# A graph network on one core: ten open building steps with idle products, a later first one-hot, and other PSUM banks for the last matrices

## The chip, the cores and the metric

The kernel runs on one core of a Trainium2 chip. The metric is the device time of one launch in microseconds, given as the median of several runs.

## The reference, cut to what matters

```python
# N=6250 nodes, E=100000 edges sorted by dst, C=256, NOUT=64, 4 layers, all float32
def agg(h):
    return jax.ops.segment_sum(h[src], dst, num_segments=N)

x0 = x
x = jnp.maximum(_layernorm(x), 0.0)
for l in range(3):
    h = x + agg(x)
    h = relu(h @ W1s[l] + b1s[l])
    h = relu(h @ W2s[l] + b2s[l])
    x = h @ W3s[l] + b3s[l]
h = x + agg(x)
h = relu(h @ cW1 + cb1)
h = relu(h @ cW2 + cb2)          # 256 -> 64
return x0 + (h @ cW3 + cb3)      # 64 -> 256
```

## The kernel before

Nodes are handled in 49 blocks of 128 (`NT`). The first matrix of a layer is applied before the sum over edges, so each layer starts from a table `z = x @ W1` that lies in DRAM and, as a high and a low part side by side, in SBUF (`XY`, 128 x 49 x 512). The sum over edges is done in two ways. For one part of the blocks, rows are gathered by an indirect DMA (`rows`, line 1427) and summed by one-hot matrices `hot` (line 1450, built by VectorE) in short TensorE products; one such block is a *visit* (class `Gathered`; `add` does the visit, `one_hots` makes its `hot`). For the other 31 blocks (the list `made`) the kernel builds a dense matrix of edge counts, block by block, and multiplies it with `XY`. The last product of a layer for such a block is preceded by a cast of the counts from bytes to numbers that TensorE reads (`a`, line 1602 in layer 0, line 1618 later).

**Building.** `build` is a generator. One of its `yield`s is one *build*: two small TensorE products (line 1114) of a low one-hot `lo` and a high one-hot `hi` into a PSUM tile `bp` (three buffers), and one cast of `bp` into the byte matrix `at`, by ScalarE (line 1122) or VectorE (line 1124). `lo` and `hi` are made by VectorE for a batch of two builds, a batch ahead, two buffers each (line 1073), from `pairs`, which ScalarE copies. A block takes 16 builds; then VectorE adds the identity to its diagonal (line 1128) and the matrix is stored to DRAM for the later layers, which read it back. There are 496 builds in all.

**The order.** Everything is issued under a schedule written out by the program: `tick` advances a step counter `now`; `later(n, fn)` runs `fn` n steps on; `job` runs between two steps, and `queue` holds the second and third matrices of each team (`mlp`). Each engine runs its instructions in the order issued. Layer 0 starts with `PRE` *open steps*, which hold two builds each and no product; `PRE` follows from `EARLY`. After them each step of layer 0 multiplies four 128-column pieces (`product_by_node`, line 1642) and holds two builds or none: the list `goals` spreads what is left of the 496 builds evenly over the steps, from `GSUB + EARLY` on. Casts `a` are made `AHEAD` = 3 steps before their product. In the open steps ScalarE makes all casts of `bp`; after `2 * PRE` builds every second one is VectorE's. A model clock (`clock`, `passed`) paces the gathers and the visits.

Right before the open steps, `looked` ends with 16 products of 128 x 512 whose result is not read (line 862). Then `layers[0].begin()` makes the first visit's `hot`, eight gathers are sent, and the open steps run. The first product of the open steps needs `pairs`, `lo` and `hi`.

**The end.** In layer 3 (`l == NLAYER`) the matrices of a team are short: 256 to 64 (`second`) and 64 to 256 (`third`, or `halves` for a team of four, two PSUM tiles). `given_out` then adds the bias and the input `x`, which it loads for the last gathered block (a team of one, block 48) in place, on VectorE: first `xt` (lines 1304, 1307, or 1300 for the last panel), then, a step later, `zz` from PSUM (line 1317), and the store. PSUM tiles `ps` come from the pool `ps_m` with two buffers. The products over panels of four blocks take `agg` tiles from another pool, `ps_a`, which has four buffers in layers 1 to 3; a panel takes two, which line 1733 (ScalarE) and, for the last panel, line 1730 (VectorE) read. `hurry` is set for the last panel of a layer and for the last gathered block.

Of the kernel before, what the change touches and what calls it, by code (L numbers as in the profile page):

```python
# [17 lines left out]
P = 128  # L18
# [378 lines left out]
def sorted_edges(  # L397
# [603 lines left out]
    with tc.manual_schedule():  # L1001
# [179 lines left out]
        def tick(layer):  # L1181

            now[0] += 1
            run = [f for t, f in due if t <= now[0]]
            due[:] = [(t, f) for t, f in due if t > now[0]]
            for f in run:
                f()
            visit = layer.meets()
            for task in list(jobs):
                first, last, fn = task  # L1190
                if max(first, lock[0]) <= now[0] and (visit or last <= now[0]):
                    jobs.remove(task)
                    fn()
            if queue:
                step(visit)
# [54 lines left out]
        def mlp(l, b0, n, h1, hurry, far):  # L1250

            w = n * P
            end = l == NLAYER
            mid = NOUT if end else C
            mp = min(mid, P)
            soon = 1 if hurry else 2
            twin = end and n % 2 == 0
            h2 = []

            def second(i):  # L1260
                if i == 0:
                    h2.append(work.tile([P, KC, W], F32, name="h2"))
                ps = ps_m.tile([P, W], F32, name="ps")
                if twin:
                    v = w // 2
                    for c in range(KC):
                        for h in range(2):
                            mm = nc.tensor.matmul(ps[h * mp:(h + 1) * mp, :v], weights[l][0][:, c, :],
                                                  h1[:, c, h * v:(h + 1) * v], start=(c == 0),
                                                  stop=(c == KC - 1))  # L1270
                        passed(v * FULL32, mm)
                    later(soon, lambda: nc.scalar.activation(
                        h2[0][:, 0, :v], ps[:, :v], AF.Relu, bias=b2[l][:2 * mp, i:i + 1]))
                    return
                for c in range(KC):
                    mm = nc.tensor.matmul(ps[:mp, :w], weights[l][0][:, c, i * P:i * P + mp],  # L1276
                                          h1[:, c, :w], start=(c == 0), stop=(c == KC - 1))
                    passed(w * FULL32, mm)
                later(soon, lambda: nc.scalar.activation(h2[0][:mp, i, :w], ps[:mp, :w], AF.Relu,  # L1279
                                                         bias=b2[l][:mp, i:i + 1]))  # L1280

            def halves():
                m, w3 = n // 2, weights[l][1]
                pss = [ps_m.tile([P, W], F32, name="ps") for _ in range(2)]
                for q in range(m):
                    for h, ps in enumerate(pss):
                        k = slice(h * mp, (h + 1) * mp)
                        mm = nc.tensor.matmul(ps[:, q * C:(q + 1) * C],
                                              h2[0][k, 0, q * P:(q + 1) * P], w3[0][k, :],
                                              start=True, stop=True)  # L1290
                    passed(C * FULL32, mm)
                for h, ps in enumerate(pss):
                    given_out(h * m, m, ps)

            def given_out(i, m, ps):
                w3 = weights[l][1]
                if b0 in inputs:
                    xs = inputs[b0][i:i + m]
                    for t in xs:
                        nc.vector.tensor_tensor(t, t, w3[1], OP.add)  # L1300
                else:
                    xt = late.tile([P, 2, C], F32, name="xt", bufs=3)
                    if b0 + i + m == NT and LAST < P:
                        nc.vector.memset(xt[:, m - 1, :], 0.0)  # L1304
                    rows_io(x, b0 + i, m, xt, True)
                    xs = [xt[:, :m, :]]
                    nc.vector.tensor_tensor(xt[:, :m, :], xt[:, :m, :],  # L1307
                                            w3[1][:, None, :].to_broadcast([P, m, C]), OP.add)
                v = ps[:, :m * C].rearrange("p (q c) -> p q c", c=C)
                z = work.tile([P, 2, C], F32, name="zz", bufs=3)  # L1310

                def add():
                    each = m // len(xs)
                    for q, t in enumerate(xs):
                        o = slice(q * each, (q + 1) * each)
                        t = t if each == m else t[:, None, :]
                        nc.vector.tensor_tensor(z[:, o, :], v[:, o, :], t, OP.add)  # L1317

                later(soon, add)
                later(soon + 1, lambda: rows_io(out, b0 + i, m, z, False))  # L1320

            def third(i):
                m = min(2, n - i)
                w3 = weights[l][1]
                ps = ps_m.tile([P, W], F32, name="ps")
                for q in range(m):
                    nodes = slice((i + q) * P, (i + q + 1) * P)
                    o = ps[:, q * C:(q + 1) * C]
                    if end:
                        mm = nc.tensor.matmul(o, h2[0][:mp, 0, nodes], w3[0][:mp, :], start=True, stop=True)  # L1330
                    else:
                        for c in range(KC):
                            mm = nc.tensor.matmul(o, h2[0][:, c, nodes], w3[:, c, :],  # L1333
                                                  start=(c == 0), stop=(c == KC - 1))
                    passed((1 if end else KC) * C * FULL32, mm)
                if end:
                    given_out(i, m, ps)
                    return
                v = ps[:, :m * C].rearrange("p (q c) -> p q c", c=C)
                z = work.tile([P, 2, C], F32, name="zz", bufs=3)  # L1340
                later(soon, lambda: nc.vector.tensor_tensor(  # L1341
                    z[:, :m, :], v, w3[:, KC:, :].to_broadcast([P, m, C]), OP.add))

                def store():
                    rows_io(tables[l + 1], b0 + i, m, z, False)
                    blocks = range(b0 + i, b0 + i + m)
                    kept.update((l, j) for j in blocks)
                    if all((l, j) in used for j in blocks):
                        split(l, b0 + i, m, z)
                    else:  # L1350
                        for j in blocks:
                            reload(l, j)
                    if sum(1 for k, _ in kept if k == l) == NT:
                        layers[l + 1].begin()
                        later(1, lambda: load_weights(l + 1))

                later(2 * soon - 1, store)

            def seconds():
                passed(BURST)  # L1360
                for i in range(-(-mid // P)):
                    second(i)

            def thirds():
                passed(BURST)
                if twin:
                    halves()
                    return
                for i in range(0, n, 2):
                    third(i)  # L1370

            wait = 1 if hurry else far - 2
            queue.append(dict(steps=[seconds, thirds], since=now[0], first=now[0] + wait,
                              last=now[0] + wait + (0 if hurry else SPAN),
                              far=2 if hurry else far, hurry=hurry))


        class Gathered:
# [28 lines left out]
                    self.upto[self.done + 1] - self.upto[1]) * self.pace  # L1407

            def begin(self):
                self.one_hots(0)  # L1410
                self.end = begun[self.l] + work_of(self.l) - TAIL[self.l]
                self.pace = (self.end - clock[0] - MARGIN) / self.upto[-1]
                self.lead = MARGIN + self.upto[1] * self.pace
                self.first = clock[0] + self.lead
# [116 lines left out]
                                     pt[:, c, :len(us) * P], AF.Relu, bias=b1[l][:, c:c + 1])  # L1531


        EARLY = 8
        PRE = (GSUB + EARLY) // 2
        tails = [7] + [panels[-1][1] + gone[-1][1]] * (NLAYER - 1) + [panels[-1][1]]
        order = [[]] + [[0, 1, 2, 19, 3, 4, 5, 6]] * 2 + [[0, 17, 1, 18, 2, 3, 19, 4, 5, 6]]
# [210 lines left out]
        with tc.tile_pool(name="hots", bufs=1) as hots, tc.tile_pool(  # L1748
# [8 lines left out]
            layers[0].begin()  # L1757
            layers[0].send(8)
            beside = build(hots, ats, ps_b)
            while now[0] < PRE:  # L1760
                for _ in range(2):
                    next(beside)
                    built[0] += 1
                tick(layers[0])
                layers[0].advance()
            later(1, lambda: later(2, lambda bad=verdict(): judge(bad)))
# [76 lines left out]
```

## Time and profile before

| what | value |
|---|---|
| median of 3 runs | 2105.08 us (2103.89 to 2105.66) |
| profiled execution: time | 2104.15 us |
| profiled execution: span | 2102.4 us |
| mean granted clock | 0.996 |
| TensorE busy | 2031.7 us, 97% |
| VectorE, ScalarE, GpSimd busy | 933.8, 879.7, 1441.1 us |

Times are in microseconds from the start of the span. PE is TensorE, PEld its weight loads, DVE VectorE, ACT ScalarE, POOL GpSimd, SP SyncE, which issues most of the DMAs. A row `out<-in` names the tiles written and read, then shapes and count. The setup takes the first 115 us, layer 0 with the building lasts until about 640 us, and layers 1 to 3 take the rest.

### The profile page before, as it was taken

Reading aid. Unit: us, or ns where it says so; the run is one execution under the profiler, and the core shown is the slowest. Engines: PE = TensorE matmul, PEld = TensorE weight load, DVE = VectorE, ACT = ScalarE, POOL = GpSimd, SP = SyncE. Lnnn points to the kernel's source line nnn. Section 1 sums busy time; section 2 is a strip of 40 time slices with the busy share of each in tenths; the row PEclk is TensorE's granted clock in tenths of the full one; section 3 lists DMA queues with packets and bytes.
Section 4 is the critical chain, followed back from the end, with each engine's and each line's share of the span. In section 5 each row is a group of like instructions: output and inputs, shape, how many; then the busy total and the mean of one; then the engine's idle time right before and its main releaser. Section 6 shows DMA issues by size and latency. Waiting matters only on the chain. (4 is left out here: it accounts for less than half of the span.)

```text
span 2102.4 us, 33308 instructions
## 1 busy us (share of the span) xinstructions
PE 2031.7 (97%) x12117; PEld 1501.4 (71%) x12117; DVE 933.8 (44%) x2108; ACT 879.7 (42%) x1799; POOL 1441.1 (69%) x1450
## 2 busy tenths in 40 slices
PE   6889999999999999999999999999999999999997
PEld 4667666666667777777777777777777777777775
DVE  5987767767673422222233322222224333333333
ACT  5866656556555523322333432323333433323331
POOL 3747777777774377777777377777777377777773
PEclk9999999999999999999999999999999999999999
DMA  5544545545554654545556555555456455656554
GB/s 166 171 136 137 158 150 154 157 150 153 155 153 145 212 163 146 169 152 179 155 174 196 186 165 149 172 159 179 147 171 202 161 179 156 196 174 206 169 171 129
DMA packets 184324, 346.92 MB, mean 165 GB/s; under 512 B 32030, under 2 KB 118080, under 8 KB 184150
## 3 DMA queue, kind: packets, MB, share of 16 engines
q0 software_dynamic: 68144, 183.13, 29.9%
q1 hardware_dynamic: 114078, 159.72, 23.1%
q8 instruction: 97, 1.59, 0.3%
q10 hardware_dynamic: 1928, 1.85, 0.3%
q14 instruction: 77, 0.63, 0.1%
HBM read 286.50 MB, written 58.07 MB: 164 GB/s over the span
## 5 line engine op out<-in xcount | busy, mean ns | idle before, releaser
L1427 POOL DMA_INDIRECT rows<-table,idx x1377 | 1381.2, 1003 | 587.5 <-issue 225.4
L1720 PE MATMUL agg<-a,XY 128*128 128x512 f32 x4116 | 976.6, 394 | 1.9 <-DVE clT L1654 1.9
L1720 PEld LDWEIGHTS agg<-a,XY 128*128 128x128 f32 x4116 | 765.2, 188 | 190.1 <-issue 32.4
L1618 ACT CAST a<-at 128x512 fp32r<-128x512 uint8 (+1 forms) x549 | 332.7, 616 | 633.2 <-PE agg L1720 591.3
L1618 DVE CAST a<-at 128x512 fp32r<-128x512 uint8 (+1 forms) x550 | 251.0, 458 | 522.4 <-PE agg L1720 476.0
L1642 PE MATMUL agg<-XY,a 128*128 128x512 f32 x1519 | 420.9, 410 | 1.7 <-ACT a L1602 1.0
L1642 PEld LDWEIGHTS agg<-XY,a 128*128 128x128 f32 x1519 | 268.3, 189 | 54.2 <-issue 9.2
L1466 PE MATMUL sums<-rows,hot 128*32 128x256 f32 x3726 | 233.4, 381 | 8.7 <-DMA rows<-table,idx 8.5
L1122 ACT CAST at<-bp 128x392 uint8<-128x392 f32 x260 | 125.0, 489 | 188.8 <-PE bp L1114 182.6
L1466 PEld LDWEIGHTS sums<-rows,hot 128*32 128x32 f32 x3726 | 118.5, 109 | 117.1 <-issue 27.6
L1602 ACT CAST a<-at 128x512 fp32r<-128x512 uint8 (+2 forms) x362 | 197.5, 575 | 4.7 <-PE agg L1642 4.7
L1124 DVE CAST at<-bp 128x392 uint8<-128x392 f32 x236 | 132.8, 563 | 133.5 <-PE bp L1114 132.7
L1495 DVE TENSOR_TENSOR u<-u,sums 128x256 f32<-128x256 f32 x81 | 33.9, 419 | 265.3 <-PE agg L1720 241.9
L1114 PE MATMUL bp<-hi,lo 128*128 128x196 bf16 x992 | 129.5, 251 | 16.9 <-DVE hi L1073 16.1
L1073 DVE TENSOR_TENSOR hi<-cols,pairs 128x784 bf16<-128x784 bf16 x248 | 139.1, 561 | 0.0
L1333 PE MATMUL ps<-w,h 128*128 128x256 f32 x588 | 135.1, 382 | 1.4 <-ACT h L1279 0.9
L1276 PE MATMUL ps<-h,w 128*128 128x512 f32 (+3 forms) x332 | 133.7, 545 | 2.0 <-DVE zz L1317 1.7
L1114 PEld LDWEIGHTS <-lo 128*128 128x128 bf16 x992 | 72.8, 98 | 87.7 <-DVE hi L1073 37.3
L1333 PEld LDWEIGHTS ps<-w,h 128*128 128x128 f32 x588 | 112.4, 192 | 18.7 <-ACT h L1279 1.3
L1073 DVE TENSOR_TENSOR lo<-lanes,pairs 128x512 bf16<-128x512 bf16 x248 | 103.6, 418 | 0.2 <-issue 0.2
L1530 ACT ACTIVATE h<-ps,bias 128x256 f32<-128x256 f32 (+1 forms) x116 | 47.5, 464 | 134.1 <-PE ps L1526 134.1
L1341 DVE TENSOR_TENSOR zz<-ps,w 128x512 f32<-128x512 f32 (+1 forms) x75 | 50.2, 678 | 117.1 <-PE ps L1333 117.1
(173 smaller groups left out, 959.0 us busy)
## 6 DMA issues: line engine op xcount, KB each, us to landing
at<-mat SPq DMA_DIRECT2D x152, 448.0 KB
mat<-at SPq DMA_DIRECT2D x31, 784.0 KB
rows<-table,idx POOLq DMA_INDIRECT x1377
table<-zz SPq DMA_DIRECT2D x72, 256.0 KB
back<-table SPq DMA_DIRECT2D x99, 128.0 KB
xs<-in_x_dram SPq DMA_DIRECT2D x8, 768.0 KB
table<-zs SPq DMA_DIRECT2D x12, 512.0 KB
out_dram<-zz SPq DMA_DIRECT2D x24, 256.0 KB
```

The lines of the kernel that those rows point to most:

```text
L1073: nc.vector.tensor_tensor(o.rearrange("p q (n t) -> p q n t", t=2), values.rearrange("p (n t) -> p n t", t=2)[:, None, :, :].to_broadcast( ...
L1114: mm = nc.tensor.matmul(bp[:, m * HW:(m + 1) * HW], lo[:, q + m, :], hi[:, q + m, :], start=True, stop=True)
L1122: nc.scalar.copy(o, v)
L1124: nc.vector.tensor_copy(o, v)
L1276: mm = nc.tensor.matmul(ps[:mp, :w], weights[l][0][:, c, i * P:i * P + mp], h1[:, c, :w], start=(c == 0), stop=(c == KC - 1))
L1333: mm = nc.tensor.matmul(o, h2[0][:, c, nodes], w3[:, c, :], start=(c == 0), stop=(c == KC - 1))
L1427: got = nc.gpsimd.indirect_dma_start(out=t, out_offset=None, in_=tables[self.l][:, :], in_offset=bass.IndirectOffsetOnAxis(ap=idx[:, o:o + ...
L1466: nc.tensor.matmul(self.sums[m * Q:(m + 1) * Q, :C], self.hot[:, c - min(rounds), m, :], self.rows[g, c + 4 * m], start=(c == ROUNDS[0][0] ...
L1602: nc.scalar.copy(a[:, i * m * P:(i + 1) * m * P].rearrange("p (j d) -> p j d", j=m), counts[b][:, j:j + m, :])
L1618: cast(o, at[:, :, d:d + m * P])
L1642: mm = nc.tensor.matmul(agg, a[:, d:d + P], XY[:, j, :], start=(j == 0), stop=(j == NT - 1))
L1720: mm = nc.tensor.matmul(agg[c][:, :w], XY[:, j, o:o + P], a[:, :w], start=(at == 0 and half == 0), stop=(at == NT - 1 and half == 1))
```

## The change

Three edits. `EARLY` goes from 8 to 4, so `PRE` goes from 12 to 10 open steps, and the products start with 20 builds done in place of 24; each open step also issues two products of 128 x 512 into a PSUM tile that nobody reads. The first visit's `hot` of layer 0 is made at step `PRE + 4` = 14, the fourth product step, in place of before the first open step. In layer 3, for teams with `hurry` (the last gathered block and the last panel), the PSUM tiles of the second and third matrices come from `ps_a` as `agg`, in place of `ps_m` as `ps`.

```diff
@@ mlp
+            def bank():
+                return (ps_a.tile([P, W], F32, name="agg") if end and hurry else
+                        ps_m.tile([P, W], F32, name="ps"))
...
             def second(i):
-                ps = ps_m.tile([P, W], F32, name="ps")
+                ps = bank()
...
             def halves():
-                pss = [ps_m.tile([P, W], F32, name="ps") for _ in range(2)]
+                pss = [bank() for _ in range(2)]
...
             def third(i):
-                ps = ps_m.tile([P, W], F32, name="ps")
+                ps = bank()
@@ Gathered
             def begin(self):
-                self.one_hots(0)
+                if self.l:
+                    self.one_hots(0)
+                else:
+                    later(PRE + 4, lambda: self.one_hots(0))
@@ sorted_edges
-        EARLY = 8
+        EARLY = 4
         PRE = (GSUB + EARLY) // 2
...
             beside = build(hots, ats, ps_b)
+            still = ps_m.tile([P, W], F32, name="ps")
             while now[0] < PRE:
                 for _ in range(2):
                     next(beside)
                     built[0] += 1
+                for _ in range(2):
+                    nc.tensor.matmul(still, XY[:, 1, :P], XY[:, 0, :], start=True, stop=True)
                 tick(layers[0])
                 layers[0].advance()
```

## The prediction

> **What bounds the kernel now.** I read the page first (engine shares), then the stage windows around the open steps, then the timeline there, then the waits of TensorE, and last the timeline and the chain of waits at the end of the span.
>
> ```profile
> span 2102.4 us, 33308 instructions
> PE 2031.7 (97%) x12117; PEld 1501.4 (71%) x12117; DVE 933.8 (44%) x2108; ACT 879.7 (42%) x1799; POOL 1441.1 (69%) x1450
> PE bp L1114 <- DVE hi L1073: 16.1, 32, 1.2
> 134.16:155.20 21.04, 21.04 (x124) 15.44 (x121) 19.26 (x45) 16.45 (x37) 13.28 (x14) 1.00 0.49 154
> ```
>
> TensorE is busy for 2031.7 of 2102.4 us, so only the 71 us in which it idles or runs slowly can be won. All of this change but its last part lies in layer 0, from 115 us on. There VectorE is nearly full too: in 134.16 to 155.20 it is busy 19.26 us beside a TensorE with no idle time. Over the whole build TensorE waits 32 times, 16.1 us in all, for VectorE's `hi`.
>
> The open steps themselves, and the first products behind them (timeline: start, length, engine, line, and in brackets the idle time before):
>
> ```profile
> 112.00 3.91 PE L862 MATMUL ps<-XY 128*128 128x512 f32 x16 [0.76 <-DVE rel L856]
> 114.76 0.96 DVE L1450 TENSOR_TENSOR hot<-colf,rel 128x768 f32<-128x768 f32 x1 [0.60 <-DMA table<-zs]
> 114.87 0.40 ACT L1068 COPY pairs<-clT 128x64 bf16<-128x64 bf16 x2 [1.74 <-DMA table<-zs]
> 115.64 0.42 DVE L1073 TENSOR_TENSOR lo<-lanes,pairs 128x512 bf16<-128x512 bf16 x1
> 115.78 1.14 POOL L1427 DMA_INDIRECT rows<-table,idx  x1 [9.43 <-DVE hot L1450]
> 116.58 0.50 PE L1114 MATMUL bp<-hi,lo 128*128 128x196 bf16 x4 [0.68 <-DVE hi L1073]
> ...
> 118.21 0.51 PE L1114 MATMUL bp<-hi,lo 128*128 128x196 bf16 x4 [0.32 <-DVE hi L1073]
> 119.03 0.52 PE L1114 MATMUL bp<-hi,lo 128*128 128x196 bf16 x4 [0.30 <-DVE hi L1073]
> ...
> 123.09 0.51 PE L1114 MATMUL bp<-hi,lo 128*128 128x196 bf16 x4 [0.30 <-DVE hi L1073]
> 123.57 0.29 DVE L1128 TENSOR_TENSOR at<-at,ident 128x128 uint8<-128x128 uint8 x1 [0.54 <-ACT at L1122]
> 124.73 0.51 PE L1114 MATMUL bp<-hi,lo 128*128 128x196 bf16 x4 [1.13 <-DVE hi L1073]
> 127.66 2.18 ACT L1602 CAST a<-at 128x512 fp32r<-128x512 uint8 x4
> 128.34 2.08 PE L1642 MATMUL agg<-XY,a 128*128 128x512 f32 x4 [1.03 <-ACT a L1602]
> ```
>
> An open step is one batch: four small products, 0.51 us, and a wait of 0.30 us for `hi`. One step follows another after 0.815 us (118.21 to 119.03, and (123.09 - 118.21) / 6). VectorE sets that pace. Once, when the first node's matrix is full, its diagonal add waits for ScalarE's casts and a step takes 1.64 us (123.09 to 124.73). The first real product starts at 128.34 us. Then the clock, by two stretches (busy time and count of TensorE, its weight loads, VectorE, ScalarE and GpSimd; then the granted clock, the DMA share and GB/s):
>
> ```profile
> 116.00:125.50 9.50, 5.14 (x40) 3.01 (x40) 8.96 (x24) 7.89 (x22) 7.67 (x7) 1.00 0.52 172
> 125.50:132.50 7.00, 5.93 (x22) 3.78 (x22) 3.84 (x11) 5.40 (x13) 1.32 (x2) 0.51 0.37 128
> ```
>
> In the open steps TensorE is busy 54% of the time; behind them, for 7 us, the granted clock is 0.51, and the first three product steps run slowly.
>
> **Hots later (-0.45 us).** Today the first VectorE instruction of the stage is the 0.96 us `hot`, and `lo` starts behind it at 115.64. Without it `lo` waits for the first of the two `pairs` copies, half of 0.40 us after 114.87, so about 115.1 to 115.2. The ends are 0 (another release that the trace hides holds `lo`) and -0.88 (it starts with 114.76). I take -0.45, because `pairs` is the one input the trace shows. `hot` issues no DMA. The gathers' first row names it as releaser (115.78); without it they start up to 1 us sooner, which nothing waits for: the first visit, paced by the planner's clock, comes where the stretch of the first fence ends, at 155.2.
>
> **Two open steps fewer (-1.63 us).** 2 x 0.815 us. The 1.64 us step stays, since its cause is the sixteenth build and both plans hold it.
>
> **Idle products (+0.2 us).** Their form stands in the trace: sixteen of them in 3.91 us, 0.244 us each. Two make 0.49 us. A warm step also needs the four small products; behind them a waiting product starts 0.30 us later (row below, 138.69 to 138.99). Together 0.79 us, in a step of 0.815 us: they fit into the wait for `hi`, with 0.02 us to spare. If the switch between the two kinds costs 0.03 us more, ten steps grow by 0.05 us each at most; I take 0.2, ends 0 and 0.5. If they ran at half clock a step would cost about 1.5 us; at a busy share near one I don't expect that.
>
> **The clock (-1.9 us).** The warm pace, from the same stage:
>
> ```profile
> 133.87 0.51 PE L1114 MATMUL bp<-hi,lo 128*128 128x196 bf16 x4
> 134.16 2.07 PE L1642 MATMUL agg<-XY,a 128*128 128x512 f32 x8
> ...
> 138.69 0.52 PE L1114 MATMUL bp<-hi,lo 128*128 128x196 bf16 x4
> 138.99 2.09 PE L1642 MATMUL agg<-XY,a 128*128 128x512 f32 x8
> 140.92 0.52 PE L1114 MATMUL bp<-hi,lo 128*128 128x196 bf16 x4
> 141.22 1.17 PE L1642 MATMUL agg<-XY,a 128*128 128x512 f32 x4
> 142.22 0.52 PE L1114 MATMUL bp<-hi,lo 128*128 128x196 bf16 x4
> ```
>
> A step with a batch takes 1.30 us (140.92 to 142.22). From 128.34 to 134.16 three such steps ran, 5.82 us against 3.90. With TensorE nearly full through the open steps I expect a granted clock of 1.00 there, so 1.92 us go. Ends: 0 (it falls cold anyway) and -1.92.
> The Trainium skill, "TensorE: Matmul & The Clock Gate", Terms, prices a cold stretch as its length times one less the clock ratio: 7.0 us x 0.49 = 3.4 us here, and the sum would be 1.5 us better; the trace bears out only 1.92, since TensorE waited for ScalarE in a part of that stretch.
> Its Part 1 says the gate closes after an idle window of some 3.4 us; the trace differs, for the longest wait of the open steps is 1.13 us (124.73), so a low busy share is enough.
>
> **Four builds moved behind (+0.6 us).** 496 builds stay 496; the four that leave the open steps come back as two batches among the products, at 0.30 us of TensorE each. Bounds: 0.6 if only TensorE counts; the next paragraph has the other end.
>
> **VectorE among the products (+0.4 us).** It gets the first `hot` at step 14, the fourth product step, and two batches with one cast each:
>
> ```profile
> L1073 DVE TENSOR_TENSOR hi<-cols,pairs 128x784 bf16<-128x784 bf16 x248 | 139.1, 561 | 0.0
> L1124 DVE CAST at<-bp 128x392 uint8<-128x392 f32 x236 | 132.8, 563 | 133.5 <-PE bp L1114 132.7
> L1073 DVE TENSOR_TENSOR lo<-lanes,pairs 128x512 bf16<-128x512 bf16 x248 | 103.6, 418 | 0.2 <-issue 0.2
> L1450 DVE TENSOR_TENSOR hot<-colf,rel 128x768 f32<-128x768 f32 x81 | 76.9, 949 | 0.6 <-DMA table<-zs 0.6
> ```
>
> 0.95 + 2 x (0.42 + 0.56 + 0.56) = 4.0 us of work. `lo` and `hi` have two buffers, so VectorE enters the products two batches ahead. A batch costs it 1.54 us at most, and some steps (138.99: eight products, no batch) bring TensorE nothing to wait for. Queued behind the moved `hot` are the next batch's one-hots and a cast that frees `bp`. I take 0.4 us as what gets through, ends 0 and 3.4 (all 4.0, with the 0.6 of TensorE inside it).
>
> **Matrices finished in the last moment (+0.3 us).** With 20 instead of 24 builds ahead, the plan of `goals` finishes the matrices of nodes 22, 26, 30 and 34 in the same step as, or one step before, the first cast that reads them; now it is two or three steps. A ScalarE cast then waits for VectorE's last cast and the 0.29 us diagonal add. The cast is made three steps ahead (`AHEAD`), 3 x 1.30 us, so a wait of 1.5 us (0.56 + 0.29 + one `a` cast, a quarter of 2.18 us, and what lies between) is covered; only ScalarE's late casts of `bp` show. Ends 0 and 4 x 1.5.
>
> **PSUM of the last matrices (0).** The end of the span:
>
> ```profile
> 2086.52 0.75 DVE L1730 TENSOR_SCALAR h<-agg,bias 128x512 f32<-128x512 f32 x1 [5.67 <-PE agg L1720]
> 2087.18 1.28 DVE L1307 TENSOR_TENSOR xt<-xt,clT 128x512 f32<-128x512 f32 x2
> 2088.39 1.28 DVE L1317 TENSOR_TENSOR zz<-ps,xt 128x512 f32<-128x512 f32 x2
> 2089.12 0.65 PE L1276 MATMUL ps<-h,w 128*64 128x128 f32 x4 [1.65 <-DVE zz L1317]
> 2089.67 0.27 DVE L1304 MEMSET xt<- 128x256 f32 x1
> 2094.17 1.21 PE L1288 MATMUL ps<-clT,h 64*128 64x256 f32 x6 [0.84 <-DVE zz L1317]
> 2090.87 2.23 DMA xt<-in_x_dram
> ```
>
> The two waits of TensorE that the change removes are there: 1.65 and 0.84 us for a `ps` that `zz` still reads. But the chain does not run over them. It goes on VectorE from 2086.52 through `xt`, `zz` and the memset, from there to the load of `x` (2.23 us) and back to VectorE, and none of these waits for L1276 or L1288 of the last panel. TensorE will be early and the end stays. The new banks are free: four `agg` banks, two held by the last panel and read before its second matrix can start. Ends: -2.1 (both waits, less 0.4 us of overlap) and 0.
>
> **The sum.** -0.45 - 1.63 + 0.2 - 1.9 + 0.6 + 0.4 + 0.3 + 0 = -2.5 us. TensorE is the bound behind layer 0's start, so it should carry to the end. The profiled execution took 2104.15 us, its span 2102.4; it lies 0.93 us below the median of 2105.08. It would become 2101.65 us, and the median **2102.6 us**.
>
> **Rivals.**
> *VectorE becomes the bound of layer 0 (slower).* Place: the products from 126 us to the end of the build. It decides from the point at which VectorE is two batches behind, so that every batch's `hi` is late. Then the clock gains nothing (in the slow steps VectorE had time to spare), all 4.0 us of its added work count in place of 1.0, and the four late matrices cost about half of their 6 us: -0.45 - 1.63 + 0.2 + 4.0 + 3.0 = +5.1, 2110.2 us. For it: 19.26 of 21.04 us busy, and the 16.1 us of waits. Against it: in the same 21 us TensorE did not wait, and VectorE has 1.8 us free there, besides the visits.
> *The tail counts (faster).* If the load of `x` or the last `zz` moves with TensorE, 2.1 us more go: -4.6, 2100.5 us. For it: both waits are real. Against it: the chain.
> *The idle products don't hold the clock (the change doesn't do what it says).* The 1.64 us step and the wait for `a` remain as gaps. Then -2.5 + 1.9 = -0.6, 2104.5 us. The Trainium skill, same page, Part 1, calls the window free-running, so the cold stretch may fall otherwise from run to run; one trace can't show that.
>
> **How the numbers follow.** Forecast 0.58, tail 0.14, clock not held 0.14, VectorE 0.14. A difference of 0.2%, 4.2 us, is about what a measurement of this kernel can tell from no change: faster means under 2100.9, slower over 2109.3. My forecast's own range is 2100 to 2105. Faster: 0.09 of the tail's case, and 0.18 from the forecast's favourable ends (hots -0.88, no VectorE cost, a longer cold stretch avoided): 0.27. Slower: most of the VectorE case, 0.12. Within 0.2%: 0.61. The range reaches from 2098.8 to 2107.2. Below: all favourable ends, the tail's among them, -0.88 - 1.63 - 1.92 + 0.6 - 2.1 = -5.9, 2099.2, less 0.4 for the scatter of runs that lie between 2103.89 and 2105.66. Above: the VectorE case with its matrices in time, -0.45 - 1.63 + 0.2 + 4.0 = +2.1.
>
> **What would show it.** Right: `lo` starts near 115.2; small products every 0.82 us with idle ones between; first product near 126.5 us; granted clock 1.00 from 112 to 140 us; the first node's 49 products done in about 15 us, not 16.7; L1276 in the tail without a wait, and yet the same distance from L1730 to the end. Wrong: a clock near 0.5 between 120 and 133 us; steps of over 0.9 us; waits for `hi` beyond 16.1 us in sum; a chain of waits whose tail begins with TensorE.

## The result

| kernel | median | runs | ratio to before, 95% interval |
|---|---|---|---|
| before | 2105.08 us | 2102.3 to 2106.15, 7 runs | |
| changed | 2097.93 us | 2096.32 to 2099.89, 7 runs | 0.9969 (0.9958 to 0.998) |
| changed, on a second chip | 2096.98 us, before there 2103.13 | 7 and 11 runs | 0.9973 (0.9962 to 0.9984) |

The change makes the kernel faster by about 6 us, where 2.5 us were predicted; 2097.93 lies 0.9 us under the low end of the range. Line numbers of the changed kernel are a few higher: the product of layer 0 is L1649 (was L1642), the panels' product L1727 (was L1720), the idle products are L1773. Ratios marked "slow chip" were measured on three chips on which the kernel before takes 2341 to 2343 us; they hold for these chips alone.

The head of the page of the changed kernel's profiled execution (2098.69 us):

```profile
span 2096.8 us, 33347 instructions
PE 2029.2 (97%) x12137; PEld 1502.2 (72%) x12137; DVE 935.8 (45%) x2110; ACT 878.4 (42%) x1797; POOL 1437.6 (69%) x1450
```

TensorE has 20 instructions more (the idle products) and yet is busy 2.5 us less. In this execution the granted clock is 1.00 from the open steps to the end; the kernel before had the cold stretch shown above and a second one, shown below. The open steps in the timeline (rows picked):

```profile
115.11 0.43 DVE L1073 TENSOR_TENSOR lo<-lanes,pairs 128x512 bf16<-128x512 bf16 x1 [0.99 <-ACT pairs L1068]
116.06 0.50 PE L1114 MATMUL bp<-hi,lo 128*128 128x196 bf16 x4 [0.19 <-DVE hi L1073]
116.34 0.71 PE L1773 MATMUL ps<-XY 128*128 128x512 f32 x2
116.90 0.52 PE L1114 MATMUL bp<-hi,lo 128*128 128x196 bf16 x4
117.19 0.71 PE L1773 MATMUL ps<-XY 128*128 128x512 f32 x2
117.75 0.52 PE L1114 MATMUL bp<-hi,lo 128*128 128x196 bf16 x4
...
124.50 0.52 PE L1114 MATMUL bp<-hi,lo 128*128 128x196 bf16 x4 [0.65 <-DVE hi L1073]
126.33 1.18 PE L1649 MATMUL agg<-XY,a 128*128 128x512 f32 x4 [0.69 <-ACT a L1609]
```

`lo` starts at 115.11, as said. The bracket of 0.30 us behind each group of small products is gone: TensorE goes from `bp` to the idle products and straight back. A step takes 0.85 us (116.90 to 117.75), 0.03 to 0.04 more than before, so the idle products do not quite fit into the wait. The first product starts at 126.33 (126.5 was predicted). The stretches of the same bounds as before, with the clock in the third place from the end:

```profile
116.00:125.50 9.50, 8.78 (x62) 5.79 (x61) 8.87 (x23) 8.35 (x22) 7.67 (x7) 1.00 0.56 182
125.50:132.50 7.00, 6.31 (x40) 4.62 (x39) 5.14 (x14) 5.91 (x13) 1.09 (x2) 1.00 0.36 114
```

TensorE is busy 8.78 of 9.5 us in place of 5.14, and the clock of the second stretch is 1.00 in place of 0.51. The end of the span, rows picked; the second block is the last `zz` of the kernel before:

```profile
2081.23 0.75 DVE L1737 TENSOR_SCALAR h<-agg,bias 128x512 f32<-128x512 f32 x1 [5.67 <-PE agg L1727]
2082.11 0.65 PE L1280 MATMUL agg<-h,w 128*64 128x128 f32 x4
2083.09 1.28 DVE L1321 TENSOR_TENSOR zz<-ps,xt 128x512 f32<-128x512 f32 x2
2084.38 0.27 DVE L1308 MEMSET xt<- 128x256 f32 x1
2085.62 1.14 PE L1292 MATMUL agg<-clT,h 64*128 64x256 f32 x8 [0.63 <-ACT h L1276]
2087.91 0.42 DVE L1311 TENSOR_TENSOR xt<-xt,clT 128x256 f32<-128x256 f32 x1 [3.26 <-DMA xt<-in_x_dram]
2090.49 1.41 DVE L1321 TENSOR_TENSOR zz<-agg,rows 128x256 f32<-128x256 f32 x4
```

```profile
2095.75 1.41 DVE L1317 TENSOR_TENSOR zz<-ps,rows 128x256 f32<-128x256 f32 x4
```

Both waits of TensorE for `zz` are gone, TensorE ends its last products 5.5 us after the relu's start (2085.62 + 1.14) in place of 8.9 (2094.17 + 1.21 against 2086.52), and the last `zz` ends 10.67 us after the relu's start, where it was 10.64 (2086.52 to 2095.75 + 1.41). TensorE is early and the end stays, as predicted.

So the two traces differ by 5.6 us in span, at these places:

| stretch | before | changed | difference |
|---|---|---|---|
| start to the first product | 128.34 | 126.33 | -2.0 |
| first product to the first product of layer 1 | 559.7 | 557.3 | -2.4 |
| from there to the last panel's relu | 1398.4 | 1397.6 | -0.8 |
| relu to the end of the span | 15.9 | 15.6 | -0.3 |

### The profile page after: what moved, and what is told of

Read it like the earlier page. It is cut to its first block, busy times and chain, and to the rows that moved or that the text cites. A ratio compares the mean times of both kernels' runs of the same rounds, so it can differ in the third digit from the quotient of the medians.

```text
span 2096.8 us, 33347 instructions
## 1 busy us (share of the span) xinstructions
PE 2029.2 (97%) x12137; PEld 1502.2 (72%) x12137; DVE 935.8 (45%) x2110; ACT 878.4 (42%) x1797; POOL 1437.6 (69%) x1450
## 3 DMA queue, kind: packets, MB, share of 16 engines
q10 hardware_dynamic: 1928, 1.85, 0.3%
## 5 line engine op out<-in xcount | busy, mean ns | idle before, releaser
L1727 PE MATMUL agg<-a,XY 128*128 128x512 f32 x4116 | 976.4, 394 | 1.9 <-DVE clT L1661 1.9
L1727 PEld LDWEIGHTS agg<-a,XY 128*128 128x128 f32 x4116 | 765.4, 188 | 189.9 <-issue 32.4
L1649 PE MATMUL agg<-XY,a 128*128 128x512 f32 x1519 | 416.2, 408 | 1.4 <-ACT a L1609 0.7
L1649 PEld LDWEIGHTS agg<-XY,a 128*128 128x128 f32 x1519 | 267.3, 189 | 50.8 <-issue 6.3
L1280 PE MATMUL ps<-h,w 128*128 128x512 f32 (+2 forms) x328 | 133.0, 548 | 0.3 <-ACT h L1740 0.3
```

What stands on the lines that cost most here:

```text
L1649: mm = nc.tensor.matmul(agg, a[:, d:d + P], XY[:, j, :], start=(j == 0), stop=(j == NT - 1))
L1727: mm = nc.tensor.matmul(agg[c][:, :w], XY[:, j, o:o + P], a[:, :w], start=(at == 0 and half == 0), stop=(at == NT - 1 and half == 1))
```

## The experiments

There are twenty traces in all. What differs on the slow chips can be seen in the waits of the weight loads: "issue" (an engine that waits for nothing that the profile shows) grows. First the changed kernel where it takes 2098 us, then where it takes 2329:

```profile
PEld sums L1473 <- issue: 28.3, 70, 0.8
```

```profile
PEld sums L1473 <- issue: 171.3, 286, 2.0
```

TensorE is also busy longer there (2149 us in place of 2029), and the mean granted clock is 0.985 in place of 0.998; the cause is not shown. In the first 140 us and the last 20 us the traces show the same pattern on all chips.

### Do the idle products hold the clock?

Three kernels: the kernel before with idle products alone, with ten open steps alone, and the changed kernel without idle products (twice).

```diff
# idle_only: the kernel before, and
+            still = ps_m.tile([P, W], F32, name="ps")
             while now[0] < PRE:
...
+                for _ in range(2):
+                    nc.tensor.matmul(still, XY[:, 1, :P], XY[:, 0, :], start=True, stop=True)
# steps_only: the kernel before, and
-        EARLY = 8
+        EARLY = 4
# no_idle: the changed kernel, and the lines that idle_only adds taken out
```

> The kernel before with two idle products in each of its 12 open steps, nothing else. If the clock is what the idle products buy: granted clock 1.00 from 112 to 140 us, open steps of 0.85 us in place of 0.815, first product 0.2 to 0.4 us later than 128.34, the first node done about 1.7 us earlier; ratio 0.9990 to 0.9995 if the stretch at 688 us stays cold, near 0.998 if it goes. If VectorE sets the pace of the first products, the first node is done at the same time as before.

> The kernel before with 10 open steps (20 builds ahead), without idle products, hot in front, PSUM as before. Sum of the prediction: first product 1.63 us earlier; the clock still falls in or behind the open steps; two batches more among the products cost 0.6 us, the late matrices 0.3. So about -0.7 us, ratio 0.9997. If the late matrices cost what VectorE's case says, +2 us, ratio 1.001.

> The changed kernel without its idle products. If they hold the clock: a cold stretch of 6.8 us comes back near 125 us and costs 1.9 us, ratio to the kernel before 0.998 to 0.999. If they do nothing, the ratio stays at 0.997 and the clock at 1.00.

> The changed kernel without its idle products, again. The cold stretch of one or two windows of 3.4 us falls between 120 and 135 us; the first node is done 1.9 us later than in the changed kernel, on a chip that gives TensorE its instructions in time the ratio is 0.9978 to 0.9988, where the changed kernel has 0.9969.

Measured, all on slow chips: idle products alone 1.0013 (0.9991 to 1.0035), steps alone 0.9964 (0.9942 to 0.9985), changed without idle products 0.9955 (0.9934 to 0.9976) and 0.9954 (0.9934 to 0.9974), beside 0.9941 and 0.9938 for the changed kernel. Steps alone were expected at 0.9997, and the changed kernel without idle products at 0.998 to 0.999: both came out lower, and these values lie outside their intervals. So on the slow chips most of the gain comes with the ten steps, more than their parts in the sum explain. The clock without idle products, in two stretches:

```profile
116.00:123.00 7.00, 4.72 (x35) 2.63 (x33) 7.00 (x18) 5.80 (x16) 5.28 (x5) 1.00 0.50 152
123.00:135.00 12.00, 9.55 (x45) 6.48 (x45) 7.80 (x20) 8.33 (x20) 4.45 (x4) 0.72 0.36 122
```

and its last small products and first real ones, rows picked:

```profile
124.97 0.83 PE L1114 MATMUL bp<-hi,lo 128*128 128x196 bf16 x4 [1.13 <-DVE hi L1073]
126.96 2.07 PE L1649 MATMUL agg<-XY,a 128*128 128x512 f32 x4 [1.03 <-ACT a L1609]
129.41 2.05 PE L1649 MATMUL agg<-XY,a 128*128 128x512 f32 x4
131.60 1.17 PE L1649 MATMUL agg<-XY,a 128*128 128x512 f32 x4
```

Four products take 2.07 us in place of 1.18. Over all twenty traces the answer has no exception: in the six without idle products the clock falls under 0.9 between 116 and 135 us (over 123 to 135 it is 0.72 in four, 0.86 and 0.57 in the others), in the fourteen with them it is 1.00. So the clock is held, as predicted. How long the cold stretch lasts differs: what the clock lacks to 1.00 in the two windows, times two, makes some 6.7 us at half clock in four traces, 3.4 in one, and 13.5 in the second trace of the kernel before (0.77 and 0.57). In time the idle products are worth 0.0015 beside ten steps on slow chips, 3.5 us, and the intervals of some 0.002 to either side of each ratio allow none. Idle products alone were expected under 1 and came out at 1.0013, an interval that takes in both. In that trace the first product comes 16.95 us after the start of the sixteen products ahead of the open steps, 16.34 before: 0.6 us later, where 0.2 to 0.4 were expected.

### One more trace of each, and the second cold stretch

> The changed kernel once more, for a second trace and a ratio beside the others. Theory CHANCE (the 6.6 us are 4.4 us of layer 0 that are always there, and some 2 us from a second cold stretch at the start of layer 1, which falls in some executions of the kernel before and not in others): ratio 0.997, again no granted clock under 0.95 from 112 to 2080 us or one such stretch at about 683 us; the visits late in layer 0 come 4.4 us earlier than before. Theory FIXED (the second cold stretch belongs to the kernel before and never to this one): the same ratio and never a cold stretch at 683 us.

> The kernel before once more, for a second trace of it. Theory CHANCE (the second cold stretch, at the start of layer 1, depends on how a window of the clock falls, not on the kernel): the wait of about 1.85 us at the first product of layer 1 is there again, and the clock behind it may be 1.00 or 0.50. Theory FIXED: it is 0.50 again, for 3.4 us. The first cold stretch, behind the open steps, is there in either theory, because TensorE is half idle for 10 us.

> The changed kernel a third time. CHANCE: behind the wait of 1.85 us at the start of layer 1 the sixteen products of 128 x 256 take 3.6 us (clock 1.00) or up to 5.1 us (clock 0.50), one or the other. The layer 0 part of the gain is there in either case.

Measured on slow chips: the changed kernel 0.9941 (0.9921 to 0.9961) and 0.9938 (0.9917 to 0.9958); the kernel before, one run, 2342.61 us. At the start of layer 1 TensorE waits 1.85 us in every kernel that leaves this place alone, but one, where it is 2.00. Behind that wait the kernel before was cold again, which the prediction does not mention. Before, then changed:

```profile
688.08 1.51 PE L1720 MATMUL agg<-a,XY 128*128 128x512 f32 x4 [1.85 <-DVE clT L1654]
689.39 5.01 PE L1333 MATMUL ps<-w,h 128*128 128x256 f32 x16
```

```profile
683.62 1.19 PE L1727 MATMUL agg<-a,XY 128*128 128x512 f32 x4 [1.85 <-DVE clT L1661]
684.65 3.62 PE L1337 MATMUL ps<-w,h 128*128 128x256 f32 x16
```

That costs 1.7 us to the end of these sixteen products, and it looks like a gain of the change. The changed kernel was warm here in all four of its traces and the kernel before cold in both of its own, so these two alone can't refute FIXED. But the kernels of the next but one section are the same code up to layer 3, and one is warm and the other cold at this place (early load, then early load without banks):

```profile
740.65 1.19 PE L1730 MATMUL agg<-a,XY 128*128 128x512 f32 x4 [1.85 <-DVE clT L1663]
741.68 3.62 PE L1339 MATMUL ps<-w,h 128*128 128x256 f32 x16
```

```profile
738.56 1.57 PE L1729 MATMUL agg<-a,XY 128*128 128x512 f32 x4 [1.85 <-DVE clT L1662]
739.93 4.95 PE L1338 MATMUL ps<-w,h 128*128 128x256 f32 x16
```

The two runs of the kernel without idle products, one and the same program, differ in the same way. Of the seventeen traces that keep this wait six are cold here, and two kernels that are the kernel before with one edit each (steps alone, `hot` later alone) are warm: CHANCE is shown for one program, and whether the kernel before falls cold here more often than the changed one is open.

### The start of layer 1 kept busy

```diff
+        for _ in range(20):
+            nc.tensor.matmul(sums[:, C:C + HW], lanes, cols, start=True, stop=True)
         for l in range(1, NLAYER + 1):
             for p in order[l]:
                 product(l, p, ps_a)
```

> The changed kernel with 20 products of 128 x 196 (bf16, constants, into the free half of the PSUM tile of the visits) right before the first product of layer 1, where TensorE waits 1.85 us for VectorE. 20 x 0.08 = 1.6 us lie inside the wait. CHANCE: the clock behind it is 1.00 in this run and in every run, which saves 1.6 us in those where it would have been cold, on average about 0.8 us of 2100: within the noise of the ratio, so the trace decides: sixteen products in 3.6 us. If the products don't fit, the first product of layer 1 waits up to 0.5 us longer.

Measured on a slow chip: 0.9936 (0.9907 to 0.9965), the changed kernel beside it 0.9938. The timeline:

```profile
740.99 1.86 PE L1786 MATMUL sums<-cols,lanes 128*128 128x196 bf16 x20
743.00 1.21 PE L1727 MATMUL agg<-a,XY 128*128 128x512 f32 x4
744.05 3.62 PE L1337 MATMUL ps<-w,h 128*128 128x256 f32 x16
```

The products lie inside the wait, and the sixteen take 3.62 us. Eleven of the seventeen traces without these products were warm too; no difference in time can be read.

### The tail: what is its chain?

```diff
# early_load: the changed kernel, and
                 if l == NLAYER and p == last and at == NT - 3:
                     bring_inputs(b0, n)
+                    bring_inputs(gone[-1][0], 1)
...
             for i, t in enumerate(inputs[b0]):
+                if b0 + i == NT - 1 and LAST < P:
+                    nc.vector.memset(t, 0.0)
# early_load_no_bank: this, and in bank()
-                return (ps_a.tile([P, W], F32, name="agg") if end and hurry else
-                        ps_m.tile([P, W], F32, name="ps"))
+                return ps_m.tile([P, W], F32, name="ps")
```

> The changed kernel with the input of the last gathered block (block 48) loaded three steps before the end of the last panel's product, beside the panel's own inputs. By the prediction's reading of the tail (the chain goes over the memset and the 2.25 us load on VectorE's queue, not over the last matrices' PSUM): the wait of 3.26 us for the load goes, the end comes 3.0 to 3.6 us sooner after the last panel's relu (12 us in place of 15.6), ratio 0.9953 on a chip where the changed kernel has 0.9969. If the end hangs on TensorE, no change.

> The same with the last matrices back in the two ps buffers, so with the banks of the kernel before. Without the load in the chain the waits of TensorE for a ps that zz still reads should count: zz of block 48 then waits for L1280 and L1334, which wait for zz, and the end comes 1 to 2 us later than with the early load and the agg banks. If the banks are worth nothing even then, the two are equal within 0.3 us from the last panel's relu on.

Measured on a slow chip: 0.9931 (0.9907 to 0.9954) and 0.9923 (0.9895 to 0.9951); no difference between them in time. Beside them on this chip ran only the changed kernel with `hot` in front, without the early load, at 0.9926: in time the early load can't be read here at all. The traces show it. Early load, rows picked:

```profile
2313.32 0.75 DVE L1740 TENSOR_SCALAR h<-agg,bias 128x512 f32<-128x512 f32 x1 [5.36 <-PE agg L1730]
2316.38 0.42 DVE L1306 TENSOR_TENSOR rows<-rows,clT 128x256 f32<-128x256 f32 x1
2318.87 1.42 DVE L1323 TENSOR_TENSOR zz<-agg,rows 128x256 f32<-128x256 f32 x4
```

Early load, banks as before, rows picked:

```profile
2310.95 0.75 DVE L1739 TENSOR_SCALAR h<-agg,bias 128x512 f32<-128x512 f32 x1 [5.37 <-PE agg L1729]
2313.55 0.65 PE L1281 MATMUL ps<-h,w 128*64 128x128 f32 x4 [1.65 <-DVE zz L1322]
2315.45 0.43 DVE L1322 TENSOR_TENSOR zz<-ps,rows 128x256 f32<-128x256 f32 x1 [1.02 <-PE ps L1335]
2318.23 1.42 DVE L1322 TENSOR_TENSOR zz<-ps,rows 128x256 f32<-128x256 f32 x4 [0.89 <-PE ps L1293]
```

From the relu's start to the end of the last `zz`: 10.67 us in the changed kernel, 6.97 with the early load, 8.70 with the early load and the old banks. The load of `x`, with its memset, was the chain, worth 3.7 us; the banks are worth nothing while it is there, and 1.7 us once it is gone, for then VectorE waits for TensorE (1.02 and 0.89 us).

### The hot in front, and later alone

```diff
# hot_front: the changed kernel, and
-                if self.l:
-                    self.one_hots(0)
-                else:
-                    later(PRE + 4, lambda: self.one_hots(0))
+                self.one_hots(0)
# hot_only: the kernel before with the opposite edit
```

> The changed kernel with the first hot back in front of the open steps. By the sum: lo starts 0.5 us later (behind the 0.96 us hot), the first product 0.5 us later, and VectorE has 0.95 us less to do among the first products. If the moved hot is free where it is now, 0.5 us slower than the changed kernel, ratio to before about 0.9972; if it costs its 0.95 us there, 0.4 us faster.

> The kernel before with the first hot at step PRE + 4 = 16, nothing else. By the sum: lo starts 0.5 us sooner, the first product 0.5 us sooner, the cold clock stays behind the open steps, so VectorE has time to spare at step 16 and the hot costs nothing there: 0.5 us faster, ratio 0.9998, within the noise of the time; the trace decides by lo's start (115.1 in place of 115.6 after the same stage) and the first product.

Measured: `hot` in front 0.9926 (0.99 to 0.9953) on a slow chip, which tells nothing beside 0.994, but in its trace the first product comes 15.06 us after the start of the sixteen products, in the changed kernel 14.37; later alone 0.9994 (0.9985 to 1.0003) where the kernel before takes 2103.68 us. In the trace of the latter, `lo` starts 0.28 us after `pairs` is begun in place of 0.77, and the first product comes 11.6 us after the first small product (11.8 before). So 0.5 to 0.7 us are gained at the front, and the clock is cold as before: 0.72 over 123 to 135 us in both. But the cold stretch lies later (0.65 over 125.5 to 132.5 us, 0.51 before) and so covers more of the products; from there to layer 1 this trace takes 560.7 us in place of 559.7. And 0.5 us in time can't be told from none.

### How much is an open step worth?

The changed kernel with another `EARLY`: 14, 12 and 11 open steps, all else as changed.

```diff
-        EARLY = 4
+        EARLY = 12      # early12_rest; 8: early8_rest; 6: early6_rest
```

> The changed kernel with 12 open steps (EARLY 8), all else as changed. PER STEP (an open step costs 0.85 us, a batch among the products 0.3 us): first product 1.7 us later than the changed kernel, layer 0 behind it 0.6 us shorter: 1.1 us slower in all, ratio 0.0005 above the changed kernel's. ORDER (the end of layer 0 is issued in another order with 12 steps, and there lies a part of the gain): layer 0 behind the first product 5 to 8 us longer than with 10 steps on these chips, ratio 0.003 above.

> The same with 11 open steps (EARLY 6). PER STEP: 0.55 us slower than the changed kernel. ORDER: as 10 or as 12 steps, by whether the last second matrix of layer 0's teams is issued before or behind the last build; the trace shows which.

> The same with 14 open steps (EARLY 12). PER STEP: 2.2 us slower than the changed kernel, first product 3.4 us later, layer 0 behind it 1.2 us shorter. ORDER: layer 0 behind the first product falls in the one or the other group, 615 to 619 us or 624 us on these chips, whatever the step count says.

> The changed kernel, for the pair with the kernel of 12 open steps. If two open steps are worth the 2.7 us that the traces of the two show (1.7 to the first product, 0.65 in layer 0 behind it, 0.3 later), ratio 0.9976; if what the first ratios show (0.9969 here against 0.9989 there) is all of it, 4.2 us, 0.9969.

These fell on chips where the kernel before takes 2103 to 2104 us:

| open steps | ratio to before, 95% interval | first product | from there to layer 1 | in it, waits for `hi` | to the last relu |
|---|---|---|---|---|---|
| 14 | 1.0006 (0.9997 to 1.0015) | 129.67 | 559.7 | 13.7 | 1398.4 |
| 12 | 0.9989 (0.998 to 0.9998) | 128.02 | 558.0 | 11.7 | 1397.7 |
| 11 | 0.9975 (0.9964 to 0.9985) | 126.77 | 560.3 | 13.5 | 1391.8 |
| 10 | 0.9973 (0.9962 to 0.9984) | 127.29 | 557.3 | 10.6 | 1394.3 |
| 12, before | 1 | 128.34 | 559.7 | 11.7 | 1398.4 |

The first product also carries up to 1.3 us by which the setup differs from execution to execution. Counted from the start of the sixteen products ahead of the open steps it comes after 17.75, 15.98, 15.18 and 14.37 us: 0.85 us a step, as PER STEP said. PER STEP had 0.55 us for a step in all. From 14 to 10 steps the ratio falls by 0.0033, 7 us, so 1.7 us a step, three times that; the intervals allow 1.0 to 2.5. In the traces 5.8 us of it stand by the start of layer 1: 3.4 at the front and 2.4 behind the first product, where PER STEP had 1.2 us the other way. ORDER isn't shown as I had it either: the stretch from the first product to layer 1 doesn't jump with a number of steps, it goes 559.7, 558.0, 560.3, 557.3. The two long stretches have the larger sums of TensorE's waits for `hi` (13.7 and 13.5 us), the two short ones the smaller (11.7 and 10.6). It does repeat for one kernel: 557.3 us in both traces of the changed kernel on such chips. What is plain is that it does not grow in step with the builds that are no longer done ahead; PER STEP had it 0.6 us longer for 10 steps than for 12, and 1.2 us longer than for 14.

The last column holds no order that the step count would explain; it differs by 3.3 us between two executions of the changed kernel (1397.6 and 1394.3). Much of it is the visits' wait for gathered rows, in these two executions:

```profile
PE sums L1473 <- DMA rows<-table,idx: 9.7, 8, 1.9
```

```profile
PE sums L1473 <- DMA rows<-table,idx: 6.7, 6, 1.7
```

The kernel with 14 steps has 9.3 us of it, that with 11 steps 2.6.

### Both edits together

The changed kernel with the early load and the busy start of layer 1.

```diff
# both: the edits of early_load and of boundary
```

> The changed kernel with the products at the start of layer 1 and the early load of block 48's input: 3.7 us from the tail, as the early load showed (6.97 us from the last panel's relu to the last zz in place of 10.66), and 0 to 1.6 us from the clock: 4 to 5 us under the changed kernel, ratio about 0.9948 where the changed kernel has 0.9969.

> The changed kernel with 20 small products at the start of layer 1 and the early load of block 48's input, again, beside the changed kernel on one chip. From the tail 3.7 us (7.0 us from the last panel's relu to the last zz in place of 10.7), from the clock 0 to 1.6 us: 4 to 5 us under the changed kernel, 10 to 12 us under the kernel before where that takes 2104 us, ratio 0.9948.

Measured: 0.9906 (0.9879 to 0.9933) on a slow chip, beside 0.9938 for the changed kernel; then 2094.71 us, 0.996 (0.9946 to 0.9974), beside 2096.98 us and 0.9973 for the changed kernel on the same chip. Relu to the end takes 11.9 us in both, 15.6 in the changed kernel: the 3.7 us are there. In the second pair's traces 2.6 us of them are lost in layers 1 to 3 (1396.9 against 1394.3), which the edits don't touch and where two executions of one kernel differ as much. The medians differ by 2.3 us, in the expected direction, and short of the expected 4 to 5; the intervals overlap. On the slow chip they differ by 6.8 us, with intervals that overlap as well.

## Why the prediction was wrong

**Hots later** -0.45: held. `lo` starts at 115.11, the first small product at 116.06 in place of 116.58, at an equal end of the setup.

**Two open steps, idle products** -1.63 + 0.2: held. With `hots` the sum to the first product was -1.9, measured -2.0. A step grew from 0.815 to 0.85 us, within the 0.05 allowed.

**The clock** -1.9: held. The kernel with 12 open steps and all else as changed shows it alone, for it has as many builds behind its first product as the kernel before. Its first product, the end of its first node, and its first product of layer 1; then the end of the first node before:

```profile
128.02 1.19 PE L1649 MATMUL agg<-XY,a 128*128 128x512 f32 x4 [0.69 <-ACT a L1609]
141.65 1.39 PE L1649 MATMUL agg<-XY,a 128*128 128x512 f32 x5
685.97 1.21 PE L1727 MATMUL agg<-a,XY 128*128 128x512 f32 x4 [1.85 <-DVE clT L1661]
```

```profile
143.83 1.39 PE L1642 MATMUL agg<-XY,a 128*128 128x512 f32 x5
```

It is 0.32 us ahead of the kernel before at the first product, 2.18 at the end of the first node, and 2.11 at the start of layer 1. So the clock is worth 1.9 us, and in the rest of layer 0 no more than 0.07 us is lost: the moved `hot` costs next to nothing among the products. That the price came out right is in part luck: it was read from one trace, and the half clock lasted from 3.4 to 13.5 us in the six cold ones. The Trainium skill's price for it, 3.4 us ("TensorE: Matmul & The Clock Gate", Terms), stays above what the trace shows. The Trainium skill's free-running window (Part 1) agrees with the second cold stretch: one and the same code was cold there in one execution and warm in another. The first stretch fell cold in all six traces without idle products; only its length and place differ.

**Builds moved, VectorE, late matrices** +0.6 + 0.4 + 0.3: this is the step that failed. The three were to give back 1.3 us among the products. Against the kernel with 12 open steps, which differs from the changed one in nothing else, the changed kernel is 1.7 us ahead at the first product, and the sum had that lead fall to 0.4 us by the start of layer 1; it grew to 2.35 (685.97 and 683.62). The term measured -0.7 in place of +1.3. The stretch from the first product to layer 1, before, with 12 steps, and changed (length, then busy time of the engines, TensorE first):

```profile
128.34:688.08 559.74, 544.32 (x3643) 384.17 (x3643) 381.85 (x868) 334.23 (x771) 387.34 (x383) 1.00 0.50 151
```

```profile
128.02:685.97 557.95, 542.50 (x3643) 382.96 (x3643) 382.53 (x869) 334.38 (x771) 388.77 (x383) 1.00 0.50 152
```

```profile
126.33:683.62 557.29, 542.60 (x3651) 383.65 (x3651) 385.14 (x875) 334.42 (x773) 383.85 (x384) 1.00 0.50 152
```

The rows of the small products in it, before and then changed:

```profile
L1114 PE MATMUL bp<-hi,lo 128*128 128x196 bf16 x944 | 122.7, 250 | 12.4 <-DVE hi L1073 11.7 <-DVE at L1124 0.2 <-ACT at L1122 0.2
```

```profile
L1114 PE MATMUL bp<-hi,lo 128*128 128x196 bf16 x952 | 123.0, 250 | 12.2 <-DVE hi L1073 11.1
```

Eight products more, where I took 0.6 us, show as 0.3 us in this line's busy time and as 0.1 us in TensorE's (542.50 and 542.60); busy times of pipelined products are too rough to tell these apart. TensorE's idle time in the stretch fell from 15.5 us (557.95 - 542.50) to 14.7, where 0.7 us more were forecast. VectorE was busy 3.3 us longer than before and kept TensorE waiting for `hi` 11.1 us in place of 11.7: its new work fell into gaps. In layer 0 TensorE waits for a cast `a` once in either kernel, 0.7 us against 1.0, and that is at the first product, so the late matrices cost it no wait. I had worked each of these out as an addition to a fixed pattern of waits; but the moved steps shift the builds against the visits and second matrices, and the pattern comes out new: 557.3 to 560.3 us over the four step counts, not in order of their builds, and long where the waits for `hi` are long. Why these waits come out longer or shorter is not shown. A term of 0.3 to 0.6 us in this stretch can't be told by adding durations, and the range should have had room for such a spread of 3.0 us.

**The tail** 0: held, and its reason is shown by the early load.

**What stays open.** The two traces differ by 5.6 us, 3.1 more than forecast. The failed step makes 2.0 of these; 1.1 lie in layers 1 to 3 and the tail and are not assigned. Layers 1 to 3 differ by 3.3 us between two executions of the changed kernel, so it may be chance. By the start of layer 1 the changed kernel is 4.5 us ahead; the ratios say 5.7 and 6.5, with intervals from 3.4 to 8.8 us that take in 4.5. A second trace of the kernel before on a chip that is not slow would be needed to say that its layer 0 repeats. Why the waits for `hi` differ with the step count as they do, and why ten steps alone are worth 0.0036 and the whole change 0.006 on a slow chip, some 14 us, is shown as a fact and not explained.

**The rivals.** VectorE as the bound is refuted by 11.1 against 11.7 us, the tail by 10.67 against 10.64, the clock not held by fourteen traces in which it stayed at 1.00.

## What to carry to other kernels

A TensorE that is half idle for some ten microseconds ahead of its main work can enter that work at half clock, as here; fill its waits with products that nobody reads, if they fit into the wait, and look at the granted clock in windows of a few microseconds, not in the page's fortieths. Before relieving a wait at the end of a kernel, follow the chain from the last instruction back: here a small load queued behind arithmetic was worth 3.7 us, and the wait that looked worse nothing until that load was gone. When an edit shifts a planned order of many small pieces, allow for a new pattern of waits on both sides, and judge parts of one or two microseconds by a stretch of the trace that repeats, not by the end.

## What had not been expected of the hardware

A TensorE busy for 54% of the time, with no wait above 1.13 us, was clocked down after about 10 us, and came back after some 7 us; in the six traces without idle products the half clock lasted some 3.4 to 13.5 us, and in one of them it began before 123 us. At the start of layer 1 a single wait of 1.85 to 2.00 us was followed by half clock in six of the seventeen traces that have it. And the same program takes 2098 us on some chips and 2329 on others, where engines stand idle without a wait that the profile shows: 171 us of "issue" at one line in place of 28.
